# Attention block with group norm on one core: q and k of 512-token blocks by one level of Strassen's algorithm, with att kept in DRAM

## The chip, the cores and the metric

The kernel runs on one core of one Trainium2 chip. The metric is the device time of one execution in microseconds, as the median of several runs. Five engines work side by side, each with a queue of its own that it executes in order: TensorE (PE in the profile; PEld is its loading of weights), VectorE (DVE), ScalarE (ACT), GpSimd (POOL) and SyncE (SP), which here issues nearly all DMAs. Matrix products land in PSUM[...]; DVE and ACT read it, POOL works in SBUF only.

## The reference

The input x is 4 images of 512 channels by 48x48 = 2304 tokens, fp32.

```python
hn = group_norm(x)                                   # 32 groups of 16 channels
qkv = einsum('oc,bchw->bohw', qkv_w, hn) + qkv_b     # 3*512 rows, fp32
q, k, v = qkv as (b, 3, 8 heads, 64, 2304) in float16
w = softmax((q * 64**-0.25) . (k * 64**-0.25))       # 2304 x 2304 for each head
a = w . v                                            # back to float32, 512 channels
out = x + proj_w . a + proj_b
```

## The kernel before, in words

Work goes by **head pairs** (4 in each image, 16 in all, g = 0 to 15) and, inside a pair, by **blocks of 512 query tokens** (`QBLOCKS`: four of 512 and one of 256). Scores are computed transposed, key tokens on the partitions. For a block and a burst of 3 x 128 keys, `scores` (L920) issues the two heads' products into three PSUM tiles of two banks and one exponential of 1024 columns on ACT for each (L939). Two bursts later, `values` (L942) multiplies them with v. `add` (L968) sums the exponentials on DVE, in f16, into `acc` (3072 columns an instruction, L986, and two folds of 1024 at a block's end, L989). When a block is done, its row sums are formed on PE (`add_up`), copied (`rows`) and sent to 128 partitions by DMA, inverted on DVE (`invert`), written to DRAM and broadcast back (`spread`), and POOL multiplies (`divide`, L1071): att, f16, kept in SBUF, one tile of all tokens for each pair (`apool`, 7 buffers). `check_sums` on POOL watches the range of the sums; a general path, which is not entered for these inputs, follows if it fails.

The main loop (L1332) runs over a **stream** of 432 slots, 27 for each pair: a slot is one burst of scores, the `add` of the burst before, the values of two bursts before, and a `fill`.

The **side work** stands in one ordered list, `beside`: q and k of later pairs, v of later pairs and images, and the output projection of the image before. An entry (`piece`) has a nominal time in us, a function, marks for the first and last piece of a chain, a condition `when`, a slot before which it may not start (`after`), and the pair that needs it (`need`). `fill` (L1283) issues from the head of the list: credit grows in each slot by the rate that the deadlines ask, and a piece is taken while the credit covers half of it. After the last piece of a chain no new chain is begun in the same `fill`, because all chains in the stream share one PSUM bank (`ps_w`, one buffer). In the slot where a block's sums are formed, `fill` comes before the values, in the others after them.

A q or k chain (`qk_steps`, L695) is, for one part and one block, 4 channel chunks x 2 halves of 64 output rows, fp32, in a bank of 512 columns, given out in two pieces of 1.7 us nominal; DVE evacuates it with bias and scale (L719). The v chains (L743) have 256 columns an instruction. The projection (L833) takes att as fp32r, which ACT casts from the f16 tile (`att32`, L821), times the weights in two parts `whi` and `wlo`. `put_convert` enters the casts, at the earliest 8 slots (`BEHIND + 6`) after the block's last slot.

Group norm of the next image is done on DVE in place on x, which stays in SBUF as tiles of 128 channels by one block (`hn[b, c, j]`), as small `tasks` in `fill`; one step of it (a power, L631) is on POOL. Pair 0's q and k and half of the first image's v come before the stream, chains back to back in several banks.

Of the kernel before, what the change touches and what calls it, by code (L numbers as in the profile page):

```python
# [467 lines left out]
def fast_path(  # L468
# [19 lines left out]
    apool = ctx.enter_context(tc.tile_pool(name="apool", bufs=2 * NPAIR - 1))  # L488
# [91 lines left out]


    alone = [True]

    def chain_bank(name):
        if alone[0]:
            return ps_s.tile([P, 2, QB], F32, tag="ps", name=name)[:, 0, :]
        return ps_w.tile([P, QB], F32, tag="pw", name=name)
# [105 lines left out]
    qk = {}  # L693
# [46 lines left out]

    vv = {}
# [40 lines left out]
    normed = {}  # L782


    atts, res, at32 = {}, {}, {}

# [34 lines left out]
    def att32(b, j, pairs=range(NC)):  # L821
        o, n = QBLOCKS[j]
        for c in pairs:
# [7 lines left out]
            nc.scalar.copy(at32[b, j, c], atts[b * NPAIR + c][:, o : o + n])  # L831
# [53 lines left out]
    def proj_pieces(b, j):  # L885
# [19 lines left out]
        return [piece(0.0, begin)], chains  # L905
# [36 lines left out]
    def values(u):  # L942
# [5 lines left out]
        if k == 0:  # L948
            if j == 0:
                atts[g] = apool.tile([P, T], F16, tag="att", name=f"att_{g}")  # L950
            av[0] = ps_av.tile([P, QB], F32, tag="av", name=f"av_{g}_{j}")
# [119 lines left out]
    def divide(g, j):  # L1071
        o, n = QBLOCKS[j]
        nc.gpsimd.tensor_tensor(  # L1073
            atts[g][:, o : o + n],
            avx.pop((g, j))[:, :n],
            ibs.pop((g, j))[:, :n],
            ALU.mult,
        )

# [3 lines left out]
    def put(pieces, after=0, need=NG):  # L1083
        for p in pieces:
            p[5], p[6] = after, need
# [36 lines left out]
    def put_qk(g, part, blocks=range(NQ)):  # L1122

        for j in blocks:
            put(qk_chain(g, part, j), (g - 2) * per_pair - 1, g)
# [13 lines left out]
    def ready(b, j):  # L1139

        if b < B - 1:
            return BEHIND + 6
# [19 lines left out]

    for b in range(B):
        g = b * NPAIR
        old = b - 1
        if b == 0:
            for j in range(NQ):
                if j < NC:
                    put_run(load_wproj, j)
                if j > 0:  # L1170
                    put_run(split_wproj, j - 1)
                put_qk(g + 1, 1, (j,))
                put_qk(g + 1, 0, (j,))
            for block in SPARE:
                put_run(reload, *block)
        put_qk(g + 2, 1)
        put_qk(g + 2, 0)

        late = [j for j in range(NQ) if (b + 1, j) in SPARE]
        early = [j for j in range(NQ) if j not in late]  # L1180
        tiles = {j: range(o // P, (o + n) // P, 2) for j, (o, n) in enumerate(QBLOCKS)}
        for j in early:
            put_v(b, 1, tiles[j])
        if b == B - 1:
            put_qk(g + 3, 1)
            put_qk(g + 3, 0, range(NQ - 1))
            put_convert(old, 0)
            put_qk(g + 3, 0, (NQ - 1,))
# [12 lines left out]
            for j in (NQ - 2, NQ - 3, NQ - 1):  # L1201
                there = ends[(NG - 2) * NQ + j] + BEHIND + 6
                put_run(att32, b, j, FIRST, after=there)
# [9 lines left out]
        for j in early:  # L1213
            if j == NQ - 1 and b > 0:
                put_convert(old, 0)
            put_qk(g + 3, 1, (j,))
            put_qk(g + 3, 0, (j,))
            put_run(reload, b + 1, j)
        for j in late:
            put_v(b, 1, tiles[j])  # L1220
            put_qk(g + 3, 1, (j,))
            put_qk(g + 3, 0, (j,))
# [7 lines left out]
        put_qk(g + 4, 1)  # L1230
        put_qk(g + 4, 0)
        put_qk(g + 5, 1)
        put_qk(g + 5, 0)
# [49 lines left out]
    def fill(n):  # L1283


# [9 lines left out]
        do_tasks(room)  # L1295
        rate, work = 0.0, 0.0
        for us, _, _, _, _, _, need in beside:
            work += us
            left = min(need * per_pair, len(stream) - 4) - n
            rate = max(rate, work / max(left, 1))  # L1300
        credit[0] = min(credit[0] + rate, 4.0)
        closed = False
        while beside:
            us, _, first, last, when, after, _ = beside[0]
# [5 lines left out]
            closed = closed or last  # L1310

# [20 lines left out]
    for n in range(end):  # L1332
        now[0] = n
        while loads and loads[0][0] <= n:
            loads.popleft()[1]()
        summed = block_at(n - BEHIND - 1)
        if summed:
# [5 lines left out]
        if summed:  # L1343

            fill(n)
        if n >= BEHIND:
# [6 lines left out]
        if block_at(n - BEHIND - 4):  # L1353
# [116 lines left out]
```

## Time and profile before

| | |
|---|---|
| time before, median of 3 runs | 1617.96 us (1617.49 to 1618.23) |
| the profiled execution: time, span | 1618.91 us, 1617.1 us |
| mean granted TensorE clock | 0.999 |
| stream of 432 slots | from about 78 us to 1597 us, 3.5 us a slot |
| scores' exponentials on ACT (L939) | 1296, 1024 ns each, 950 ns apart |
| sum of exponentials on DVE (L986) | 349, 1750 ns each |
| att product on POOL (L1073) | 78, from 722 to 2822 ns |
| DMA | 82.1 MB, SP's queue 17.3% of the 16 engines |

The profile is one execution. In a row of instruction groups, "busy" is the time in which at least one of the group was at work, "mean ns of one" the mean duration, and the last part the idle time of that engine just before, with what ended it. In the timeline a row is: start in us, length in us, engine, line, operation, names written <- read, shapes, count, and in brackets the idle time before. The ends of matmuls are modelled; their starts are measured. Each fp32 matmul of the code appears as two instructions.

### The profile page before, as it was taken

To read this page: it belongs to the slowest core of one execution; us is meant where nothing else is said; L and a number is where in the kernel's file an instruction comes from. 1 tells how busy PE (TensorE), PEld (TensorE's weight loads), DVE (VectorE), ACT (ScalarE), POOL (GpSimd) and SP (SyncE) were. 2 spreads that over 40 slices of the span, in tenths; PEclk is the share of its full clock that TensorE was granted. 3 is DMA by queue.
4 is the path that set the end of the run, shared out by engine and by line. 5 is a ranking of instruction groups with operands and counts; after the bars stand their busy time and mean duration, and the time that the engine had idled before them with its cause. 6 is when DMAs were issued, how large, how long until landed. Compare 5 with 4: busy or idle time off the path is not lost.

```text
span 1617.1 us, 28315 instructions
## 1 busy us (share of the span) xinstructions
PE 1583.4 (98%) x11500; PEld 695.5 (43%) x11500; DVE 1136.2 (70%) x1302; ACT 1282.8 (79%) x1398; POOL 298.4 (18%) x419
## 2 busy tenths in 40 slices
PE   6999999999999999999999999999999999999996
PEld 2533434443333534555333353455533334434544
DVE  6267668866666678986666666898666666767775
ACT  3077777888888888888887887887888888888894
POOL 1001102211121222212111121111211131111211
PEclk9999999999999999999999999999999999999999
DMA  7002020000000023511000002352100000016424
GB/s 221 1 14 66 11 64 24 18 14 11 14 18 14 12 65 118 154 54 28 14 11 18 14 12 61 100 158 73 31 14 12 14 18 15 15 24 191 121 62 132
DMA packets 94898, 82.11 MB, mean 51 GB/s; under 512 B 50852, under 2 KB 60964, under 8 KB 94756
## 3 DMA queue, kind: packets, MB, share of 16 engines
q1 hardware_dynamic: 92724, 78.35, 17.3%
q8 instruction: 92, 1.51, 0.4%
q10 hardware_dynamic: 1904, 1.84, 0.4%
q14 instruction: 50, 0.41, 0.1%
q0 software_dynamic: 128, 0.01, 0.0%
HBM read 60.70 MB, written 19.17 MB: 49 GB/s over the span
## 4 chain that ended last, share of the span: by engine, by line
PE 91%; ACT 4%; issue 2%; DVE 1%; DMA 1%; POOL 0%; SPq 0%; ACTq 0%; DVEq 0%; POOLq 0%
PE pqk L709 29%; PE ps L932 19%; PE av L957 19%; PE pv L760 16%; PE pr L837 7%; ACT p L939 3%; PE ps L709 1%; PE sl L1009 1%; ACT a L831 1%; DMA x<-x_dram 1%; DVE acc L986 0%; DMA sums<-slx 0%; DVE r L860 0%; DMA row<-inv 0%; DMA ib<-row 0%
## 5 line engine op out<-in xcount | busy, mean ns | idle before, releaser
L939 ACT ACTIVATE p<-ps 128x1024 f16<-128x1024 f32 x1296 | 1231.9, 1027 | 299.9 <-PE ps L932 299.3
L986 DVE TENSOR_TENSOR acc<-acc,p 128x3072 f16<-128x3072 f16 x270 | 485.3, 1798 | 75.5 <-ACT p L939 74.7
L709 PE MATMUL pqk<-x,wqkv 128*64 128x512 f32 (+1 forms) x2464 | 519.3, 551 | 0.0
L932 PE MATMUL ps<-q,k 64*128 64x512 f16 (+1 forms) x2880 | 359.5, 358 | 6.2 <-ACT p L939 5.3
L957 PE MATMUL av<-p,v 128*64 128x512 f16 (+1 forms) x2880 | 361.0, 364 | 0.4 <-DVE slx L1025 0.3
L760 PE MATMUL pv<-wqkv,x 128*64 128x256 f32 x2304 | 268.6, 380 | 0.0
L709 PEld LDWEIGHTS pqk<-x,wqkv 128*64 128x64 f32 x2464 | 168.9, 137 | 224.2 <-issue 166.8
L1047 POOL TENSOR_SCALAR in<-sums 128x8 f32<-128x8 f32 (+1 forms) x158 | 116.6, 738 | 795.0 <-DMA sums<-slx 788.7
L932 PEld LDWEIGHTS <-k 64*128 64x128 f16 x2880 | 107.3, 94 | 286.1 <-issue 238.1
L957 PEld LDWEIGHTS <-v 128*64 128x64 f16 x2880 | 131.9, 109 | 210.8 <-issue 166.6
L1073 POOL TENSOR_TENSOR att<-avx,ib 128x512 f16<-128x512 f32 (+1 forms) x78 | 120.0, 1539 | 450.4 <-DMA ib<-row 406.3
L760 PEld LDWEIGHTS pv<-wqkv,x 128*64 128x64 f32 x2304 | 160.1, 137 | 92.8 <-issue 4.5
L986 DVE TENSOR_TENSOR acc<-p,p 128x3072 f16<-128x3072 f16 x79 | 138.2, 1749 | 0.0
L837 PE MATMUL pr<-a,whi 128*128 128x512 f32 (+1 forms) x312 | 122.2, 399 | 4.6 <-DVE r L860 3.2
L837 PE MATMUL pr<-a,wlo 128*128 128x512 f32 (+1 forms) x312 | 114.4, 373 | 0.0
L989 DVE TENSOR_TENSOR acc<-acc 128x1024 f16<-128x1024 f16 x156 | 108.4, 695 | 5.4
L719 DVE TENSOR_SCALAR q<-pqk,bqkv 128x512 f16<-128x512 f32 (+1 forms) x79 | 55.0, 696 | 80.4 <-PE pqk L709 79.8
L719 DVE TENSOR_SCALAR k<-pqk,bqkv 128x512 f16<-128x512 f32 (+1 forms) x75 | 52.2, 696 | 78.1 <-PE pqk L709 78.0
L768 DVE TENSOR_TENSOR v<-pv,bv 128x512 f16<-128x512 f32 x72 | 49.7, 691 | 81.1 <-PE pv L760 80.9
L966 DVE COPY avx<-av 128x512 f32<-128x512 f32 (+1 forms) x79 | 50.6, 641 | 66.4 <-PE av L957 66.4
L864 DVE SCALAR_TENSOR_TENSOR r<-pr,bproj,r 128x512 f32<-128x512 f32 (+1 forms) x80 | 54.9, 694 | 43.6 <-PE pr L837 43.0
L837 PEld LDWEIGHTS pr<-a,whi 128*128 128x128 f32 x312 | 58.5, 187 | 41.9 <-issue 18.7
(62 smaller groups left out, 448.8 us busy)
## 6 DMA issues: line engine op xcount, KB each, us to landing
r<-x_dram SPq DMA_DIRECT2D x72, 256.0 KB, 3.0
out_dram<-r SPq DMA_DIRECT2D x69, 256.0 KB, 2.1
ib<-row SPq DMA_DIRECT2D x126, 128.0 KB, 3.0
x<-x_dram SPq DMA_DIRECT2D x62, 256.0 KB, 4.3
x<-x_dram SPq DMA_DIRECT2D x16, 128.0 KB, 4.8
sums<-slx SPq DMA_DIRECT2D x128, 2.0 KB, 2.1
ib<-row SPq DMA_DIRECT2D x30, 64.0 KB, 3.0
wqkv<-qkv_wT_dram SPq DMA_DIRECT2D x2, 768.0 KB, 6.9
```

What stands on the lines that cost most here:

```text
L709: nc.tensor.matmul(pw[0][lo : lo + D, :n], wqkv[:, c, w0 + lo : w0 + lo + D], hn[b, c, j], start=(c == 0), stop=(c == NC - 1),)
L719: nc.vector.tensor_scalar(qk[g][part][:, o : o + n], pw[0][:, :n], bqkv[:, col : col + 1], SCALE, ALU.add, ALU.mult,)
L760: nc.tensor.matmul(pw[0][lo : lo + D, a, :], hn[b, c, i * P // QB][:, at + lo : at + lo + D], wqkv[:, c, 2 * C + half * C // 2 :][:, : C / ...
L837: nc.tensor.matmul(ps[:, :n], w[:, c, bass.ts(m, P)], at32[b, j, c], start=(i == 0), stop=(i == len(steps) - 1),)
L864: nc.vector.scalar_tensor_tensor(xt[:, i], places[i], bias, xt[:, i], ALU.add, ALU.add)
L932: nc.tensor.matmul(ps[:, h, a * n : (a + 1) * n], kt[rows, bass.ts(i, P)], qt[rows, o : o + n], start=True, stop=True,)
L939: nc.scalar.activation(pt[:, r], ps, AF.Exp)
L957: nc.tensor.matmul(av[0][lo : lo + D, :n], vv[b, pr // 2][:, i, pr % 2 * P + lo : pr % 2 * P + lo + D], pt[:, r, h, a * n : (a + 1) * n], ...
L986: nc.vector.tensor_tensor(t, before, pt, ALU.add)
L989: nc.vector.tensor_tensor(t[:, 0], t[:, 0], t[:, r], ALU.add)
L1047: nc.gpsimd.tensor_scalar(t, sm, limit, None, op)
L1073: nc.gpsimd.tensor_tensor(atts[g][:, o : o + n], avx.pop((g, j))[:, :n], ibs.pop((g, j))[:, :n], ALU.mult,)
```

## The change

For pairs 1 to 15, q and k of a 512-token block are no longer two chains of four chunks. The weights of q and k (2 x 128 rows by 512 channels) and the block of x (512 channels by 2 x 256 tokens) are taken as 2 x 2 matrices of blocks, and the four result blocks (q and k, each for the first and the second 256 tokens) come from seven products of 128 rows x 256 channels x 256 tokens, in Winograd's form: four sums of weights for each pair (`weight_sums`), four differences of x for each block (`x_sums`), both on POOL, and seven additions in the evacuation, by ACT, DVE and POOL. Two products share the bank at a time: `one` (p1, p2), `two` (p6, p7), `three` (p5, p3), and `four`, which takes p4 of two blocks. The 256-token block of each pair is computed as before, with q and k in one bank (`small_pieces`). q and k of a pair are entered in three groups of blocks (`GROUPS`), each piece a chain of its own.

Differences are prepared by `prepare` at the end of a `fill`, up to two items, at most one block ahead of the block whose turn it is; `ready_for` issues what is missing before the product that needs it. In a slot where `fill` comes after the values, a second `fill` is done before them if the credit is above 2.6. The credit's growth has moved into `pace`, once a slot.

att of all pairs but the last goes from POOL into a small f16 tile and by SP to DRAM; one tile of 512 columns by 4 chunks, `attl`, is fetched back for each block before `att32`, one fetch at a time. The division runs 5 slots after a block's values end in place of 4, and the casts start after `BEHIND + 9` slots in place of `BEHIND + 6`. The SBUF of `apool` goes from 7 buffers to 1, and holds the new tiles.

```diff
-    apool = ctx.enter_context(tc.tile_pool(name="apool", bufs=2 * NPAIR - 1))
+    apool = ctx.enter_context(tc.tile_pool(name="apool", bufs=1))
...
+    def weight_sums(g):
+        a11, a12, a21, a22 = (w_of(g, part, up) for part in (0, 1) for up in (0, 1))
+        s = [
+            work.tile([P, 2, P], F32, tag=f"s{i}", bufs=1, name=f"s{i}_{g}")
+            for i in range(4)
+        ]
+        nc.gpsimd.tensor_tensor(s[0], a21, a22, ALU.add)
+        nc.gpsimd.tensor_tensor(s[2], a11, a21, ALU.subtract)
+        nc.gpsimd.tensor_tensor(s[1], s[0], a11, ALU.subtract)
+        nc.gpsimd.tensor_tensor(s[3], a12, s[1], ALU.subtract)
...
+    def x_sums(k, which):
...
+            t = work.tile([P, 2, HALF], F32, tag=f"t{which}", name=f"t{which}_{g}_{j}")
...
+        for c in range(2):
+            nc.gpsimd.tensor_tensor(t[:, c], ins[0][c], ins[1][c], ALU.subtract)
...
+    def free(k, which):
+        if which == 0:
+            return k == 0 or (k - 1, 3) in sent
+        return k < 2 or (k - 2, {1: 3, 2: 4, 3: 2}[which]) in sent
...
+    def product(to, w, xs):
+        for c in range(2):
+            for lo in (0, D):
+                nc.tensor.matmul(
+                    to[lo : lo + D, :],
+                    w[:, c, lo : lo + D],
+                    xs[c],
+                    start=(c == 0),
+                    stop=(c == 1),
+                )
...
+        def scaled(engine, to, ps, other):
+            engine.scalar_tensor_tensor(to, ps, SCALE, other, ALU.mult, ALU.add)
+        def one(i, j):
...
+            p1, p2 = two_banks(f"p12_{g}_{j}")
+            product(p1, w_of(g, 0, 0), x_of(g, j, 0, 0))
+            product(p2, w_of(g, 0, 1), x_of(g, j, 1, 0))
...
+            nc.scalar.activation(t1, p1, AF.Identity, bias=bq[:, col], scale=SCALE)
+            scaled(nc.vector, qk[g][0][:, o : o + HALF], p2, t1)
+        def two(i, j):
+            k = first + i
+            ready_for(k, 2)
+            p6, p7 = two_banks(f"p67_{g}_{j}")
+            product(p6, weights[g][1], halves_of(parts[k, 2]))
+            product(p7, weights[g][2], halves_of(parts[k, 3]))
+            sent[k, 2] = True
+            x_sums(k, 4)
...
+            scaled(nc.vector, u2, p6, parts[k, "t1"])
...
+            nc.scalar.activation(u, p7, AF.Identity, bias=bkq[:, col], scale=SCALE)
+            nc.gpsimd.tensor_tensor(u, u, u2, ALU.add)
+        def three(i, j):
...
+            product(p5, weights[g][0], halves_of(parts[k, 1]))
+            product(p3, weights[g][3], x_of(g, j, 1, 1))
...
+            nc.scalar.activation(c5, p5, AF.Copy, scale=SCALE)
+            scaled(nc.vector, u4, p5, parts[k, "u2"])
+            scaled(nc.vector, qk[g][0][:, o : o + HALF], p3, u4)
...
+            nc.gpsimd.tensor_tensor(qk[g][1][:, o : o + HALF], c5, u, ALU.add)
+        def four():
+            banks = two_banks(f"p4_{g}_{js[0]}")
+            for i, p4 in enumerate(banks):
+                product(p4, w_of(g, 1, 1), halves_of(parts[first + i, 4]))
...
+            scaled(
+                nc.vector,
+                to[:, :, :HALF],
+                last_bank[0].rearrange("p (a t) -> p a t", a=2),
+                u3[0].rearrange("p (a t) -> p a t", a=2),
+            )
...
+    def fetch(b, j):
+        o, n = QBLOCKS[j]
+        t = work.tile([P, NC, QB], F16, tag="attl", bufs=1, name=f"attl_{b}_{j}")
+        pairs = NC - 1 if b == B - 1 else NC
+        nc.sync.dma_start(
+            t[:, :pairs, :n],
+            atd[b].rearrange("(c p) t -> p c t", p=P)[:, :pairs, o : o + n],
+        )
...
     def divide(g, j):
...
+            to = work.tile([P, QB], F16, tag="att", name=f"att_{g}_{j}")[:, :n]
         nc.gpsimd.tensor_tensor(
-            atts[g][:, o : o + n],
...
+            to, avx.pop((g, j))[:, :n], ibs.pop((g, j))[:, :n], ALU.mult
         )
+        if g < NG - 1:
...
+            at = atd[b][pr * P : (pr + 1) * P, o : o + n]
+            loads.append((now[0] + 1, lambda: nc.sync.dma_start(at, to)))
...
         if b < B - 1:
-            return BEHIND + 6
+            return BEHIND + 9
...
         if summed:
             fill(n)
+        elif beside and credit[0] > 2.6:
+            fill(n, False)
         if n >= BEHIND:
             values(stream[n - BEHIND])
```

## The prediction

> **What bounds the kernel now.** I read the page first: busy shares, chain, groups.
>
> ```profile
> PE 1583.4 (98%) x11500; PEld 695.5 (43%) x11500; DVE 1136.2 (70%) x1302; ACT 1282.8 (79%) x1398; POOL 298.4 (18%) x419
> ...
> PE 91%; ACT 4%; issue 2%; DVE 1%; DMA 1%; POOL 0%; SPq 0%; ACTq 0%; DVEq 0%; POOLq 0%
> ```
>
> TensorE (PE) is busy for 98% of the span and carries 91% of the chain that ended last; its own waits come to some 24 us, half of them one wait at the start. A matmul saved shortens the run, as long as no other engine makes PE wait. POOL is nearly free.
>
> A busy time cannot price a matmul, because matmuls overlap. I price them by the spacing of the evacuations in the opening, where chains run back to back (timeline of the first 110 us):
>
> ```profile
> 41.73 0.75 DVE L719 TENSOR_SCALAR q<-pqk,bqkv 128x512 f16<-128x512 f32 x1 [2.68 <-PE pqk L709]
> ...
> 45.16 0.75 DVE L719 TENSOR_SCALAR q<-pqk,bqkv 128x512 f16<-128x512 f32 x1 [2.68 <-PE pqk L709]
> ...
> 57.24 0.69 DVE L768 TENSOR_TENSOR v<-pv,bv 128x512 f16<-128x512 f32 x1 [2.76 <-PE pv L760]
> 60.70 0.69 DVE L768 TENSOR_TENSOR v<-pv,bv 128x512 f16<-128x512 f32 x1 [2.76 <-PE pv L760]
> ```
>
> A q chain is 4 chunks x 2 halves of 64 output columns, and the trace has two instructions for each fp32 matmul: 16 instructions of 512 columns in 3.43 us, 215 ns each. A v chain is 32 instructions of 256 columns in 3.45 us, 108 ns each. So 256-column instructions with the same 64-column fp32 weights, which is what the change issues, cost half: their weight loads stay hidden.
>
> Then one slot of the stream in the middle of q and k work (timeline, 374 to 392 us):
>
> ```profile
> 386.57 2.85 ACT L939 ACTIVATE p<-ps 128x1024 f16<-128x1024 f32 x3 [0.44 <-PE ps L932]
> ...
> 386.83 0.84 PE L957 MATMUL av<-p,v 128*64 128x512 f16 x6
> ...
> 387.50 1.88 PE L709 MATMUL pqk<-x,wqkv 128*64 128x512 f32 x8
> ...
> 389.32 0.82 PE L932 MATMUL ps<-q,k 64*128 64x512 f16 x6
> 389.44 0.75 DVE L719 TENSOR_SCALAR q<-pqk,bqkv 128x512 f16<-128x512 f32 x1 [1.52 <-PE pqk L709]
> 389.75 2.85 ACT L939 ACTIVATE p<-ps 128x1024 f16<-128x1024 f32 x3 [0.32 <-PE ps L932]
> ```
>
> A slot is three score tiles, one piece of side work and the value matmuls of two slots before. With one piece (8 instructions of 512, about 1.72 us) it lasts 3.24 us (386.08 to 389.32); in it ACT works 2.85 us and waits 0.32 to 0.44 us for scores. That 0.4 us is all the room ACT has. DVE starts on a chain only after its last matmul, and its sum of 1.75 us sits in the same queue.
>
> The last reading is how POOL and DVE stand to each other (timeline, 300 to 330 us):
>
> ```profile
> 317.45 1.75 DVE L986 TENSOR_TENSOR acc<-acc,p 128x3072 f16<-128x3072 f16 x1
> ...
> 317.73 2.60 POOL L1073 TENSOR_TENSOR att<-avx,ib 128x512 f16<-128x512 f32 x1 [4.22 <-DMA ib<-row]
> ...
> 319.12 1.69 DVE L660 TENSOR_SCALAR x<-x,ga,gb 128x256 f32<-128x256 f32 x2
> ```
>
> The POOL product needs 1.27 us alone. Here it takes 2.60: it starts during DVE's sum (which ends at 319.20) and gets 1.13 us of progress only afterwards. Then the two DVE instructions queued at 319.12 take 1.69 us in place of 0.73.
>
> **What the Trainium skill says.** *SBUF — State Buffer*, "Who interferes with whom": a VectorE instruction with two SBUF inputs, or in a two-port mode, and a GpSimd instruction that reads SBUF exclude each other, and the second waits for the whole of the first. The lines above agree: 1.33 us lost. *GPSIMD Engine Reference*, "3.1 Elementwise — side-by-side cycle accounting": a two-input GpSimd operation needs about 2.6 cycles an element. Trace: 732 ns for 256 columns, 1267 for 512, so 2.09 ns an element and 197 ns fixed, a little better. *ScalarE: Activation LUTs*, "What ACT_TABLE_LOAD costs": 186 ns + 0.833 ns a column, 93 more for each pointer operand, 93 of overlap between neighbours. Trace: 585 by that rule for the 256-column normalisation with two pointers, 586 measured. *TensorE: Matmul & The Clock Gate*, "Wait — 56ns, not 53.3ns?": columns / 2.4 + 2.5 ns; 215.8 and 109.2 against the 215 and 108 above.
>
> **The change, part by part.**
>
> *Matmuls.* Fifteen head pairs (all but the first) have four 512-token blocks each: 60 blocks. Before: 2 parts x 16 instructions of 512 = 32 x 215 = 6.87 us. After: 7 products x 2 chunks x 2 halves x 2 = 56 instructions of 256, 56 x 108 = 6.04 us. Saved 0.83 us x 60 = **50 us**, all on PE. The 256-token blocks keep their matmuls and only share a bank.
>
> *ACT.* Three 256-column evacuations a block (t1, u, c5), by the skill's rule 493, 493 and 399 ns, less the overlap 400, 400, 306: 1.1 us x 60 = +66 us. No row prices an activation from PSUM of this size; the nearest, the 256-column cast from SBUF, is 421 ns. Bounds: 0.3 to 0.5 us each. Most new chains carry one, so ACT does 2.85 + 0.37 = 3.22 us in a slot of 3.24. It is hidden by a hair; 2 chains in 14 ("four") carry none and the v and projection slots give room back, and three score banks let ACT lag some 0.7 us. Over the run: 1283 + 66 = 1349 of about 1580, 85%.
>
> *DVE.* Per block it loses 2 evacuations of 750 ns and gets four of 256 columns, two-input from PSUM, 478 ns (the row of the 256-column residual), and half of one of 512 (750): 1.50 becomes 2.29 us, x 60 = +47 us, to 1183. Hidden by PE, until waits on POOL are added.
>
> *POOL.* Per block 8 differences and 2 sums of 256 columns, and 4 weight sums a pair: 660 x 0.73 = +480 us, to about 780 without waits. A slot of 3.24 us has 5/6 of a 1.75 us sum, 0.23 us of folding and some 0.1 us of normalisation on DVE's side: about 1.8 us taken. POOL wants 10 x 0.57 us in 6.5 slots, plus the division and check (1.6 us in 6), about 1.15 of the 1.4 us left. It fits, with about 20% to spare. Cost to DVE: an add that finds POOL at work waits up to 0.57 us; about 500 such instructions x 0.2 = 100 us, so DVE comes to 1280 of 1580, 81%.
>
> *New waits.* All side chains share one PSUM bank. Before, a 512 chain held it over two slots; now a chain fills and is emptied within each. After "one" the bank is free only after ACT's t1 (behind three exponentials) and a DVE step, about 1.0 us after the chain's end; the next chain starts 1.4 us after it (386.08 to 387.50 in the trace). So 0.4 us of slack, 0.1 after "three" (two DVE steps). Behind a late DVE step stands the next sum, then the next evacuation. Where the new second fill puts a chain before the values, the other follows within 0.8 us and must wait about 0.7. Pieces: 29.5 of 1.72 us in 27 slots a pair, so doubles are few. Between pairs POOL must do 4 weight sums and 6 differences after the old pair's last "three" and before the new pair's first "two", five slots on: 10 operations at about 2.5 a slot. Bounds for all this: 0 to 0.35 us a chain over 210 chains (0 to 73 us), of which I take 0.07 (15 us); 0 to 2 us at each of 15 pair changes (0 to 30), of which I take 0.4 (6 us). No reason suggests a gain here.
>
> *att through DRAM.* 75 stores of 128 KB or less and 20 fetches of up to 512 KB join SP's queue: 18 MB more on 82, DMA share 17% to 21%, 95 issues of about 0.4 us. The division runs one slot later and its store a slot after that, the sums' DMA a slot later again, so SP is held only if POOL is over a slot late; then DVE's reciprocal, which waits for the sums, is held too. Converts start three slots later (9 for 6), covered by other pieces where the queue has any; two slots are given to each fetch, against 3 to 5 us for loads of 256 KB. Taken as 0, bounds 0 to 10 us. The group scale's power on POOL (0.7 us) now stands behind differences: 0 to 3 us, three times, taken as 0. The last pair's att stays in SBUF, so the end is unchanged.
>
> Sum: -50 + 15 + 6 = -29 us on the profiled execution's 1618.9 (span 1617.1 + 1.8 around it), 1590. The median shown is 1 us below that execution, within rounding: **1590**.
>
> **Rivals.** (1) *Everything hides.* PE stalls for no more than now: 1618 - 50 = 1568, with a few doubles 1573. For it: the slack of each stage is positive by the numbers above. Against: four engines end within 0.4 us of each other in a slot. (2) *The shared port turns the bound over.* POOL's differences delay DVE's sums, these delay evacuations, and PE waits at the single bank before each chain, or at "two" for differences that POOL has not finished. The saving is spent at 50 / 210 = 0.24 us a chain; a full wait for one POOL operation (0.57 us) less the 0.25 us of slack, 0.32 us, gives 67 us of stalls: 1635. For it: the 2.60 and 1.69 us above. Against: before, the 63 products of 512 columns already average 1691 ns for 1267, and PE shows no wait that leads to them. (3) *ACT saturates.* If its step takes 0.55 us, a slot is 3.4 us rather than 3.24: 0.16 x 180 = 29 us on top, 1619 with my stalls, no change. (4) *The saving is not there*, because 256-column products do not run at 108 ns: against it stand 2304 such v instructions.
>
> **How the numbers follow.** Forecast case (1578 to 1606) 0.48; everything hides, below 1578, 0.22; ACT or DVE taking most of the saving, 1606 to 1622, 0.13, a third of it within 0.2% (3.2 us, about what a measurement of this kernel can tell from no change); the shared port, above 1622, 0.17. Faster 0.76, same 0.05, slower 0.19. The range runs from 1571 (all hidden) to 1628, into the port case.
>
> **What would show it.** Right: 32 x 60 instructions of 512 replaced by 56 x 60 of 256 near 108 ns, PE's busy time down by about 50 us and its share down to 96 or 97%; ACT near 1350, POOL near 800, DVE sums on average 0.1 to 0.3 us longer. Wrong: PE waits for DVE evacuations or for POOL's differences of over 50 us in sum, or ACT without gaps through the q and k slots.

## The result, and the profile after

| | before | after |
|---|---|---|
| time, median | 1617.87 us (1617.49 to 1618.23) | **1761.7 us** (1757.91 to 1766.51) |
| ratio, 95% interval | | **1.0891** (1.0864 to 1.0918): slower |
| profiled execution: time, span | 1618.91, 1617.1 us | 1762.06, 1760.1 us |
| mean granted TensorE clock | 0.999 | 0.978 |
| stream of 432 slots, start of the first to start of the last | 1516.5 us | 1662.1 us |

Forecast were 1590 us, with a range of 1571 to 1628; the run is 144 us slower than before. First the busy shares of the changed kernel (the page's first part):

```profile
PE 1590.8 (90%) x12940; PEld 826.9 (47%) x12940; DVE 1231.6 (70%) x1452; ACT 1342.0 (76%) x1578; POOL 1010.2 (57%) x1082
```

PE went from 98% of its span to 90%. ACT's 1342 us and DVE's 1232 us are what the prediction summed up (1349, 1183 to 1280), and neither is full: the bound has not passed to another engine. PE has become an engine that waits. (The chain of what ended last can be followed back over only 1% of this span; what follows rests on waits, timeline and slots.)

The waits of the changed kernel: engine, instruction, what ended the wait; us in sum, times, longest.

```profile
DVE u4q L863 <- ACT p L907: 97.6, 52, 3.0
...
ACT u3k L893 <- DVE u2q L863: 75.4, 57, 6.8
...
DVE q L863 <- ACT t1q L876: 52.8, 45, 2.9
PEld p L835 <- ACT u3k L893: 41.6, 33, 2.7
...
PE p L835 <- DVE q L863: 36.3, 35, 6.2
...
PE p L835 <- ACT u3k L893: 25.2, 19, 2.2
...
PE p L835 <- POOL t L797: 4.7, 4, 1.8
```

ACT and DVE wait for one another inside one evacuation, and products (`p`, L835) wait for the last step of the evacuation of the pair of products before. They hardly wait for the differences themselves (4.7 us, and 11.1 us before their weight loads).

Now the timeline, a slot of undisturbed length and the long one after it:

```profile
449.13 4.44 POOL L797 TENSOR_TENSOR t<-x,x 128x256 f32<-128x256 f32 x2
...
450.99 0.82 PE L1185 MATMUL ps<-q,k 64*128 64x512 f16 x6
451.04 1.94 DVE L1239 TENSOR_TENSOR acc<-acc,p 128x3072 f16<-128x3072 f16 x1
451.21 0.47 ACT L893 ACTIVATE u3k<-p,bkq 128x256 f32<-128x256 f32 x1 [0.42 <-DVE u2q L863]
...
453.52 1.27 POOL L1331 TENSOR_TENSOR att<-avx,ib 128x512 f16<-128x512 f32 x1
...
454.24 0.82 PE L1185 MATMUL ps<-q,k 64*128 64x512 f16 x6
...
454.83 0.33 SPq L1338 DMA_DIRECT2D attd<-att  x1
...
456.53 0.38 SPq L1070 DMA_DIRECT2D attl<-attd  x1
457.01 1.14 SPq L1281 DMA_DIRECT2D sums<-slx  x2
...
460.95 0.20 DVE L1307 RECIPROCAL inv<-sums 128x8 f32<-128x8 f32 x1 [7.97 <-DMA sums<-slx]
...
461.51 0.42 DVE L863 SCALAR_TENSOR_TENSOR q<-p,u4q 128x256 f16<-128x256 f32 x1
...
462.08 3.68 PE L835 MATMUL p<-x,wqkv 128*64 128x256 f32 x16 [6.25 <-DVE q L863]
```

The slot from 450.99 to 454.24, with 16 instructions of 256 columns, lasts 3.25 us: as long as the 3.24 us with 8 instructions of 512 before, so the price per instruction is right. The trouble begins in it. Two differences take 4.44 us (449.13 to 453.57) in place of 1.4 because DVE's sums hold the port. Behind them POOL's att product (453.52) is late. The store of att stands in SP's queue ahead of the sums' DMA and leaves only at 454.83; a fetch of att between the two then waits for that store to land (456.53). So the sums' DMA is issued only at 457.01, DVE's reciprocal waits 7.97 us for it, and behind the reciprocal in DVE's queue stands the evacuation that PE needs: in the next slot PE waits 6.25 us.

The 16 instructions after the wait then last 3.68 us in place of 1.89, at half the clock. The table by stretches of the changed kernel, "us, busy us of PE, PEld, DVE, ACT, POOL, PEclk, DMA share, GB/s":

```profile
446.00:459.00 13.00, 9.69 (x84) 4.84 (x79) 5.09 (x5) 10.62 (x13) 12.21 (x13) 1.00 0.13 31
459.00:465.50 6.50, 3.42 (x16) 1.92 (x16) 2.62 (x4) 0.00 (x0) 4.29 (x7) 0.50 0.27 83
```

The Trainium skill, *TensorE: Matmul & The Clock Gate*, "What's actually happening", says that an idle window of about 3.4 us halves TensorE's clock and that a busy one restores it. The trace agrees on the half clock and on the length: in the stream there are 14 spells at 0.50, 3.4 or 6.8 us each, 68 us in sum; before there is none. It differs on how much idling is needed. The spells begin on a fixed grid of 3.41 us; in the stretch of 3.41 us just before each of them the profile has PE idle for 1.8 to 3.2 us, and in no other full-clock stretch of the stream for more than 1.7. So a wait of some 2 us can be enough, and it is then paid again in part: here 3.42 us of PE work at half clock, 1.7 us lost on top of the 6.25. In all the spells PE was at work for 52.5 us; half of that, about 26 us, is my estimate of what they cost the stream.

The groups that answer to the lock shown before (busy, mean ns of one):

```profile
L1239 DVE TENSOR_TENSOR acc<-acc,p 128x3072 f16<-128x3072 f16 x270 | 504.5, 1869 | 30.0 <-ACT p L1192 29.4
...
L797 POOL TENSOR_TENSOR t<-x,t 128x256 f32<-128x256 f32 x240 | 257.4, 1093 | 112.1 <-PE p L835 111.6
...
L1242 DVE TENSOR_TENSOR acc<-acc 128x1024 f16<-128x1024 f16 x156 | 149.6, 959 | 5.4
```

Alone a difference takes 0.72 us, here 1093 ns or more on average. DVE's sums went from 1798 to 1869 ns on average (the 1750 ns ahead of the prediction is the median), the folds from 695 to 959, the first sum of a block from 1749 to 1843: 270 x 71 + 156 x 264 + 79 x 94 ns = 68 us lost on DVE.

### The profile page after: what moved, and what is told of

Read it like the earlier page. It is cut to its first block, busy times and chain, and to the rows that moved or that the text cites. A ratio compares the mean times of both kernels' runs of the same rounds, so it can differ in the third digit from the quotient of the medians.

```text
span 1760.1 us, 32708 instructions
## 1 busy us (share of the span) xinstructions
PE 1590.8 (90%) x12940; PEld 826.9 (47%) x12940; DVE 1231.6 (70%) x1452; ACT 1342.0 (76%) x1578; POOL 1010.2 (57%) x1082
## 5 line engine op out<-in xcount | busy, mean ns | idle before, releaser
L1239 DVE TENSOR_TENSOR acc<-acc,p 128x3072 f16<-128x3072 f16 x270 | 504.5, 1869 | 30.0 <-ACT p L1192 29.4
L1185 PE MATMUL ps<-q,k 64*128 64x512 f16 (+1 forms) x2880 | 369.0, 360 | 13.2 <-ACT p L1192 11.3
L797 POOL TENSOR_TENSOR t<-x,t 128x256 f32<-128x256 f32 x240 | 257.4, 1093 | 112.1 <-PE p L835 111.6
L1300 POOL TENSOR_SCALAR in<-sums 128x8 f32<-128x8 f32 (+1 forms) x158 | 95.8, 606 | 342.9 <-DMA sums<-slx 334.3
L835 PE MATMUL p<-t,s 128*64 128x256 f32 x1440 | 180.9, 386 | 40.3 <-ACT u3k L893 25.2
L1242 DVE TENSOR_TENSOR acc<-acc 128x1024 f16<-128x1024 f16 x156 | 149.6, 959 | 5.4
L835 PEld LDWEIGHTS p<-t,s 128*64 128x64 f32 x1440 | 102.2, 138 | 108.1 <-ACT u3k L893 41.6
L1239 DVE TENSOR_TENSOR acc<-p,p 128x3072 f16<-128x3072 f16 x79 | 145.6, 1843 | 0.9 <-ACT p L1192 0.9
L797 POOL TENSOR_TENSOR t<-x 128x256 f32<-128x256 f32 x120 | 134.5, 1140 | 0.0
L835 PE MATMUL p<-x,wqkv 128*64 128x256 f32 x960 | 117.5, 387 | 16.5 <-DVE q L863 13.0
L797 POOL TENSOR_TENSOR t<-x,x 128x256 f32<-128x256 f32 x120 | 131.0, 1111 | 1.6 <-DVE x L668 1.6
```

The source lines that it names most:

```text
L797: nc.gpsimd.tensor_tensor(t[:, c], ins[0][c], ins[1][c], ALU.subtract)
L835: nc.tensor.matmul(to[lo : lo + D, :], w[:, c, lo : lo + D], xs[c], start=(c == 0), stop=(c == 1),)
L1185: nc.tensor.matmul(ps[:, h, a * n : (a + 1) * n], kt[rows, bass.ts(i, P)], qt[rows, o : o + n], start=True, stop=True,)
L1239: nc.vector.tensor_tensor(t, before, pt, ALU.add)
L1242: nc.vector.tensor_tensor(t[:, 0], t[:, 0], t[:, r], ALU.add)
L1300: nc.gpsimd.tensor_scalar(t, sm, limit, None, op)
```

## The experiments

They take the change apart. Each time is the median of two or four executions, each ratio is to the kernel before on the same chip (1618.4 to 1618.9 us). Lengths of stretches, slots and waits come from the one profiled execution of each kernel.

### First: one suspect at a time

**Plain chains.** In `group_pieces`:

```diff
-        return wino_pieces(g, js) if len(js) == 2 else small_pieces(g, *js)
+        return [p for j in js for part in (1, 0) for p in qk_chain(g, part, j)]
```

> The change with its q and k put back to plain chains (two of 512 columns for each block); att in DRAM, the later casts, the second fill and the pace stay. Three theories for the 192 us by which the stream of slots is longer than its matmuls ask. A (the store): att's store stands in SP's queue until POOL, late with differences of x, has divided; the DMA of the next block's sums is behind it, DVE waits for the sums and everything waits for DVE. B (POOL's load): the differences are not ready or keep the shared port from DVE. C (the bank): ACT and DVE read one bank in turn, so each waits in its queue for the other, and the one bank comes free late. All three need the seven products: each expects 1620 to 1640 here, the old time and a few us for the fetches at the end. If att in DRAM were itself the cause, the time would stay above 1690.

Measured: 1680.4 us, 1.0381 (1.035 to 1.0411). Without anything of Strassen, the rest of the change (att in DRAM, later casts, second fill, `pace`) costs 62 us. The prediction took it as nothing.

**Store of att later**, so that SP doesn't hold the sums' DMA behind a late POOL:

```diff
-            loads.append((now[0] + 1, lambda: nc.sync.dma_start(at, to)))
+            stores.append((now[0] + 5, lambda: nc.sync.dma_start(at, to)))
...
-            return BEHIND + 9
+            return BEHIND + 13
```

(fetches four slots later too)

> The change with att's store issued five slots after the division in place of one (fetches and casts four slots later accordingly), so that POOL has divided before SP comes to the store and nothing stands behind it. A: DVE's waits for the sums (34 us in 7 pieces) go, with the slow-clock spells after them: 1700 to 1720. B and C: only the late divisions are gone, within 15 us of 1762.

Measured: 1753.7 us, 1.0833 (1.0791 to 1.0876), against 1.0891 (1.0864 to 1.0918). SP's waits, of the changed kernel and of this one:

```profile
SPq L1338 <- POOL att L1331: 501.3, 69, 19.1
```

```profile
SPq L1339 <- POOL att L1332: 21.4, 5, 7.3
```

480 us of SP's waiting go and the run gains 8, with intervals that overlap. Two effects cancel in this. In pairs 1 to 13 (slots 27 to 377) the stream is 23.6 us shorter than in the changed kernel, and DVE's waits for the sums fall from 34.0 us (7 times) to 8.2 (3 times). From the last pair's first slot to the end the run is 12.8 us longer: the first of the last five fetches is issued in slot 416 in place of 412, so that slots 412 to 415 have no side work and the projections are bunched behind them. So the hold shown at 454.83 costs some 24 us of the stream, an estimate that the run's total hides; it is a twentieth of what SP waits in sum.

**No differences.** The products read blocks of x where the change reads differences:

```diff
...
-        for c in range(2):
-            nc.gpsimd.tensor_tensor(t[:, c], ins[0][c], ins[1][c], ALU.subtract)
-        parts[k, which] = t
+        parts[k, which] = x_of(g, j, which > 2, which % 2)
```

> The change without the differences of x: the products take blocks of x in their place, and the scale of q and k is a quarter, so q and k are not the reference's, and the check of the sums has no consequence. POOL loses 480 of its 660 new instructions; matmuls, ACT and DVE stay. B: the products and DVE's sums no longer wait for POOL: 1580 to 1620. A: POOL divides in time, so the gain is that of the late store and little more: 1690 to 1720. C: bank and evacuations are as they were, so 1690 to 1720 as well, with PE's waits for DVE and ACT before products still there.

Measured: 1695.8 us, 1.0475 (1.0445 to 1.0506): the differences cost 66 us.

**Evacuations on DVE**: t1, u and c5 by `nc.vector.tensor_scalar` in place of `nc.scalar.activation`.

> The change with t1, u and c5 evacuated by DVE in place of ACT, so that DVE alone reads the bank. C: the waits of ACT for DVE (75 us) and of DVE for ACT (150 us) go, the bank is free sooner and the time falls to 1690 to 1720, although DVE does 70 us more. A and B: DVE's extra work makes it no better, 1760 to 1790.

Measured: 1759.8 us, 1.0871 (1.0839 to 1.0902): no difference. Taking these steps off ACT gains nothing where DVE takes them up.

### Second: the schedule, and the number of steps

**Casts ahead.** The cast of att before a projection is marked as the last piece of a chain, so that the projection isn't released in the same fill; on plain chains and on the change (the three early casts of the last image likewise):

```diff
-        return [piece(0.0, begin, when=when)], chains
+        return [piece(0.0, begin, last=True, when=when)], chains
```

> Plain chains with att in DRAM (1680), and the cast entered as the last piece of its fill, so that its projection starts one slot later at the earliest. Theory D (the cast): since the cast waits for a fetch, it and its projection are let go in one fill, and PE stands behind the cast, which stands behind three exponentials on ACT: some 3 us of waiting, and after it 3 to 7 us at half the clock, at each of 20 fetches. D expects 1625 to 1650. Rival: the fetches themselves come too late (one buffer, one fetch at a time), PE runs out of side work in the last pair whatever the order: 1665 to 1680.

> The change itself with the cast entered as the last piece of its fill. D: the same gain as with plain chains, 30 to 50 us: 1710 to 1730. Rival (fetches too late): within 15 us of 1760.

Measured: 1668.4 us, 1.0305 (1.0265 to 1.0344) on plain chains, 12 us less than without; 1751.7 us, 1.0819 (1.0788 to 1.0851) on the change, 10 less. The place is the last pair. In the changed kernel:

```profile
1644.71 1.70 ACT L1061 CAST a<-attl 128x512 fp32r<-128x512 f16 x3
1645.42 0.79 PE L1089 MATMUL pr<-a,whi 128*128 128x512 f32 x1 [2.86 <-ACT a L1061]
...
1646.43 0.36 SPq L1070 DMA_DIRECT2D attl<-attd  x1
1646.44 0.63 PE L1089 MATMUL pr<-a,whi 128*128 128x512 f32 x1
1646.87 0.63 PE L1089 MATMUL pr<-a,wlo 128*128 128x512 f32 x1
```

PE waits 2.86 us for the first cast, and the projection then runs at half clock (some 425 ns from one start to the next; 233 from 1650.26 on).

**One evacuation.** No differences, and each pair of products emptied by one DVE `tensor_scalar` of 512 columns:

> The kernel without differences (1696), and each pair of products evacuated whole by one DVE instruction of 512 columns, as a plain chain is; t1, u, c5, the sums on POOL and the further DVE steps are left out, so q and k are not the reference's. Left are the seven products in chains of one slot each. Theory C (the hand-over of the bank, ACT after exponentials and DVE after ACT, comes later than the next chain's start): 1630 to 1645, 62 us of it att in DRAM less 48 us of matmuls. Rival: a chain in every slot on one bank is too tight by itself, whoever empties it: 1675 to 1695.

Measured: 1646.4 us, 1.0169 (1.0139 to 1.0198), 49 us less than with the steps.

**No second fill** in the change:

```diff
-        elif beside and credit[0] > 2.6:
-            fill(n, False)
```

> The change without the second fill ahead of the values. C: two chains in one slot wait for the bank, so taking them away gains 5 to 20 us unless the work that is left over piles up at the pairs' ends, where it is issued without pause. Rival: that pile costs more: 1765 to 1800.

Measured: 1721.8 us, 1.0634 (1.0603 to 1.0665): 40 us for two lines. The trace has 11 slots without any side work in the change, 5 without the second fill. Seven of the 11 lie in the last pair (five of them in slots 417 to 428), where only projections are left and none is released before its fetch is two slots old; two of the 5 do. Of the 43 us by which the stream is shorter, the last pair gives back 25. The first pair gives 12: with the second fill its slots 5 and 17 hold two chains of products each and last 7.0 and 7.1 us, where in the kernel before a slot with two pieces takes 4.96.

### Third: the ladder, all without the second fill

> Plain q and k chains of 512 columns, att in DRAM with its store, fetch and later casts, and no second fill before the values: against the kernel before, only att in DRAM and the bookkeeping of the rate remain. The question is whose the 62 us of the plain chains (1680) were. Theory A, the second fill: it spends the side work early and leaves the slots of the last pair bare, and a pair's late casts are then waited for; without it the stream is again even and the run takes 1618 to 1630. Theory B, the transfer of att: stores and fetches in SP's queue and casts that wait for them cost most of the 62, and the run stays at 1655 to 1680.

> The seven products alone: no differences and no sums of x or u on POOL, each pair of products emptied by one DVE instruction of 512 columns (the other steps of the combination are left out, so q and k are not the reference's), no second fill. Theory of the schedule: with the second fill, the differences and the steps gone, the 50 us of matmuls should appear: about the time of plain chains without the second fill less 46 to 50, so 1570 to 1585 if that one is near 1620. Rival, the shorter chains themselves (a bank filled and emptied within a slot, 14 groups where there were 8) cost PE time: 1600 to 1630.

> No differences of x on POOL (the products take blocks of x in their place, so q and k are not the reference's), evacuations in steps as in the change, no second fill. If the costs add, 1696 - 40 = 1656 us, and the steps of the evacuation are then worth this run less the one with one evacuation (expected about 50 to 70). If the second fill's cost was mostly a collision with POOL's lateness, the gain without it is under 25 us here: 1670 or more.

| kernel, each without the second fill | us | ratio (95%) | step |
|---|---|---|---|
| before | 1618.9 | | |
| plain chains, att in DRAM | 1636.4 | 1.0107 (1.009 to 1.0124) | +17.5 |
| seven products, one evacuation, no differences | 1606.6 | 0.9923 (0.9907 to 0.994) | -29.8 |
| the same, evacuation in steps | 1653.2 | 1.0217 (1.02 to 1.0234) | +46.6 |
| with the differences (the run above) | 1721.8 | 1.0634 (1.0603 to 1.0665) | +68.6 |
| with the second fill (the change) | 1761.7 | 1.0891 (1.0864 to 1.0918) | +39.9 |

The terms hardly depend on each other: the second fill costs 44 us on plain chains, 40 with one evacuation, 43 without differences; the differences 66 with it and 69 without; the steps 49 and 47. The saving is there: the row with one evacuation beats the kernel before by 0.8%, though it leaves most of the combination out. The next row, still without the differences, has lost it.

Where the steps lie in the stream, read from the traces: mean length of a slot, from its first score product to that of the next slot, for slots with the same work (number of them in the change's schedule in brackets; side work of 16 instructions of 256 columns or 8 of 512).

| | one q and k piece (173) | one v piece (91) | block's end, one q and k piece (30) |
|---|---|---|---|
| before | 3.24 | 3.26 | 3.46 |
| plain chains | 3.24 | 3.26 | 3.49 |
| one evacuation | 3.29 | 3.27 | 3.70 |
| in steps | 3.44 | 3.26 | 4.13 |
| with differences | 3.55 | 3.39 | 4.89 |

The steps cost 173 x 0.15 + 30 x 0.43 = 39 of the 47 us; the differences 173 x 0.11 + 91 x 0.13 + 30 x 0.76 = 54 of the 69. The slots at a block's end, where `fill` stands before the values, lose most each. The timeline of the kernel in steps without differences:

```profile
920.39 1.95 PE L821 MATMUL p<-x,wqkv 128*64 128x256 f32 x16
921.94 2.37 DVE L1228 TENSOR_TENSOR acc<-acc 128x1024 f16<-128x1024 f16 x2
...
922.43 0.47 ACT L862 ACTIVATE t1q<-p,bq 128x256 f32<-128x256 f32 x1 [0.36 <-PE p L821]
...
924.23 0.41 DVE L849 SCALAR_TENSOR_TENSOR q<-p,t1q 128x256 f16<-128x256 f32 x1
...
924.70 1.95 PE L821 MATMUL p<-x,s 128*64 128x256 f32 x16 [0.84 <-DVE q L849]
```

The chain's products end at 922.27, t1 is ready at 922.90, but DVE is in two folds, lengthened to 2.37 us by POOL's att product, and takes its step at 924.23; PE waits 0.84 us for the bank.

**Three mends of the schedule together** (no second fill, cast ahead, store later) on the change:

> The change as it is, with three edits of its schedule: no second fill, casts entered as a last piece so that a projection is not released in the same fill, the store of att four slots later. Alone these gave 40, 10 and 8 us. If they are separate costs the run takes about 1762 - 58 = 1704; if the second fill was behind the other two (the late casts of the last pair are the same gaps), 1715 to 1722.

Measured: 1711.6 us, 1.0576 (1.0558 to 1.0594): 50 us less than the change, 10 less than without the second fill alone. The later fetches take back a part here too: against the run without the second fill, pairs 1 to 13 are 20.9 us shorter, the last pair and the end 8.0 longer. It is the fastest run of the whole change, and still 93 us behind the kernel before. A later store without later fetches at the end was not tried.

### Fourth: how the differences and the steps cost

**Differences made, but read by nobody**, and **POOL as busy, but only writing**:

```diff
-        parts[k, which] = t
+        made[k, which] = t
+        parts[k, which] = x_of(g, j, which > 2, which % 2)
```

```diff
-        for c in range(2):
-            nc.gpsimd.tensor_tensor(t[:, c], ins[0][c], ins[1][c], ALU.subtract)
+        nc.gpsimd.memset(t, 1.0)
+        nc.gpsimd.memset(t, 1.0)
+        nc.gpsimd.memset(t[:, 0], 1.0)
```

> The change without the second fill (1721.8 us), with the differences of x made on POOL as before but read by nobody: the products read blocks of x, so q and k are not the reference's. Theory of the port: POOL's reading makes DVE wait and DVE's evacuations come late; nothing changes for that here, so 1700 to 1722. Rival, the products wait for differences (and POOL for products before it may overwrite them): it goes to within 10 us of the run without differences, 1653 to 1665.

> As the run with unread differences, but each pair of differences of 2 x 726 ns is replaced by three fills of a constant (512, 512 and 256 elements; from the rows of 8 and 96 elements 563 + 563 + 350 = 1476 ns): POOL is as busy and as late for its other work, but it reads nothing. Theory of the port: most of the cost goes, 1655 to 1675, and DVE's sums come back from 1870 to about 1790 ns. Rival, POOL's lateness (att, its store, SP's queue, the reciprocal behind it): the cost stays, 1690 to 1720.

Measured: 1719.3 us, 1.0622 (1.0595 to 1.0649), unread; 1660.2 us, 1.0265 (1.0248 to 1.0282), writing only. Nobody needs the differences here and they cost as much as ever, 66 us over the kernel without them (1653.2); with the same instructions' time spent in writing, 7. So what costs is POOL's reading of SBUF. DVE's groups, first of the kernel with unread differences, then of the one that only writes:

```profile
L1242 DVE TENSOR_TENSOR acc<-acc,p 128x3072 f16<-128x3072 f16 x270 | 509.9, 1889 | 27.1 <-ACT p L1195 26.4
L1245 DVE TENSOR_TENSOR acc<-acc 128x1024 f16<-128x1024 f16 x156 | 150.7, 966 | 5.4
```

```profile
L1243 DVE TENSOR_TENSOR acc<-acc,p 128x3072 f16<-128x3072 f16 x270 | 486.9, 1803 | 30.6 <-ACT p L1196 30.1
...
L1246 DVE TENSOR_TENSOR acc<-acc 128x1024 f16<-128x1024 f16 x156 | 127.8, 819 | 5.3
```

The rows are back at those of the kernel without differences (1788 and 821 ns). The Trainium skill, *SBUF — State Buffer*, "Who interferes with whom", says just this: a VectorE instruction with two SBUF inputs contends with a GpSimd one that reads SBUF, not with one that only writes. What stays open is by which way the 59 us between the two runs reach PE. The fills aren't lengthened themselves (three in 532 + 528 + 316 = 1376 ns, against 2 x 1.1 us), so POOL is also less late for its other work: SP's waits for its att product fall from 489 to 375 us, and DVE's for the sums from 33.0 to 15.1. That way, through SP's queue, costs some 21 us beside the differences, by the run with three mends; the rest may be DVE's late steps.

**The same subtractions beside plain chains**: 480 of 256 columns (of weights, read by nobody), one or two at the end of each slot from the 27th on.

```diff
+        if n >= 27:
+            for i in range((n - 26) * 480 // 405 - (n - 27) * 480 // 405):
+                t = work.tile([P, HALF], F32, tag="t9", bufs=2, name=f"t9_{n}_{i}")
+                a, z = wqkv[:, i, :HALF], wqkv[:, i + 2, :HALF]
+                nc.gpsimd.tensor_tensor(t, a, z, ALU.subtract)
```

> Plain q and k chains, att in DRAM, no second fill (1636.4 us), and 480 POOL subtractions of 256 columns (of two blocks of weights, read by nobody), one or two at the end of each slot from the 27th on. Theory that POOL's reads delay every DVE result that PE waits for: as beside the products, 1690 to 1705. Rival, they cost that much only where a bank is filled and emptied within a slot by several steps; a chain of 16 instructions over two slots has some 1.4 us of room: 1640 to 1660.

Measured: 1655.5 us, 1.0219 (1.0202 to 1.0236), 19 us over plain chains. DVE's rows:

```profile
L1239 DVE TENSOR_TENSOR acc<-acc,p 128x3072 f16<-128x3072 f16 x270 | 512.5, 1898 | 61.9 <-ACT p L1192 61.3
L1242 DVE TENSOR_TENSOR acc<-acc 128x1024 f16<-128x1024 f16 x156 | 145.8, 934 | 5.4
```

Over plain chains without them (1778 and 712 ns) DVE loses 270 x 120 + 156 x 222 ns = 67 us, no less than beside the short chains (270 x 101 + 156 x 145 + 79 x 116 ns = 59 us). The same delay of DVE goes with 66 us where each slot fills and empties the bank, and with 19 where a chain runs over two slots: its slots stay at 3.24 us. The comparison isn't clean. The subtractions here are spread evenly and those of the change come in bunches, and SP's waits for POOL hardly rise here (249 us, 241 without the subtractions), so that the hold in SP's queue, some 21 of the 66 us, is missing. How much of the rest is the bunching wasn't tried.

**Steps on DVE** (t1, u, c5; no differences, no second fill), and **steps without POOL's two sums** (c5 goes straight to k, u is not summed):

> Seven products, no differences, no second fill, evacuation in steps (1653.2 us), with t1, u and c5 on DVE instead of ACT. q and k are not the reference's, since blocks of x stand for the differences. Theory of the order on one bank: DVE's steps no longer wait behind ACT's exponentials (92 + 50 us of such waits) nor ACT for DVE (42 us); ACT loses 58 us of work and DVE gains some 65; the run gains 15 to 40: 1613 to 1638. Rival, the number of steps in a row at the bank and DVE's load: no gain, 1645 to 1665.

> Seven products, no differences, no second fill, evacuation in steps (1653.2 us), with POOL's two sums a block left out: c5 goes from ACT straight to k, and u is not summed (q and k are not the reference's). 120 POOL operations of 1.35 to 1.6 us go. Theory of the port, at the price of the differences (59 us for 480 operations, 0.12 us each): 15 us gained, 1638. Rival, the bank's hand-over from engine to engine is the whole cost: 1649 to 1655.

Measured: 1653.5 us, 1.022 (1.0203 to 1.0237), and 1645.9 us, 1.0155 (1.0135 to 1.0175), against 1653.2 us with both. On DVE the plain slots get shorter (3.36 for 3.44 us), which fits ACT and DVE waiting for each other there, but block ends get longer (4.52 for 4.13), probably because all steps now stand behind the folds: my expected 15 to 40 us failed. POOL's sums are worth 7 us (half of the price that I had from the differences). What stays, 39 us, is the price of several steps in a row at one bank, on whichever engine; the number of steps and the work queued ahead of each were not separated.

**Plain chains with the store later and casts ahead**, no second fill:

> Plain chains with att in DRAM and no second fill (1636.4 us), with the store four slots later and each cast a last piece. If the 17 us are SP's queue and projections released together with their casts, 1620 to 1628; if they are the later casts themselves (9 slots after a block for 6, thinner side work at the image changes), 1632 to 1642.

Measured: 1640.4 us, 1.0134 (1.0117 to 1.0151): no gain on 1636.4, with intervals that overlap. Again two effects cancel. The stream is 11.8 us shorter than without the two edits and only 4.4 us longer than before; but what follows the start of its last slot takes 39.2 us in place of 24.1 (22.8 before), since the last fetches come about four slots later and more of the projection is left over (66 instructions after that start, for 24). In pairs 1 to 13 the edits gain 2.4 us, so SP's hold and the release in one fill cost little there with plain chains. Without the two edits the stream is about 17 us longer than before in pairs 2, 6 and 9 to 11 and 6.6 us in the last, and a little shorter elsewhere. Whether later casts, the transfers or the new `pace` make the 17.5 us stays open.

## Why the prediction was wrong, point by point

The sum was -50 + 15 + 6. Its first term holds; what failed is the price of everything around the matmuls. The waits at the bank and for POOL, taken as 21 us, cost about 135: some 20 for the shorter chains, 46.6 for the steps, 68.6 for the differences. Two terms were put at nothing: the second fill, which cost 39.9 us, and att through DRAM, 17.5.

- **Matmuls, -50 us: right.** Undisturbed slots with 16 instructions of 256 columns are as long as those with 8 of 512, and the step from plain chains to seven products is -29.8 us though it already has shorter chains in one bank (slots of 3.29 for 3.24 us, block ends of 3.70 for 3.49).
- **Durations of the new instructions: right or a little high.** t1 and u take 473 ns and c5 407 (taken: 493 and 399), the two-input steps about 0.42 us (478), a difference 0.72 alone (0.73). DVE's lock waits came to 68 us (about 100 taken). The sums of ACT and DVE held, and said little about the time. POOL came to 1010 us rather than 800.
- **The signs named beforehand.** PE's busy time was to fall by about 50 us; it rose from 1583.4 to 1590.8, and the half clock is some 26 of the 58 us between. PE's waits for evacuations before products, 36.3 + 25.2 us in the rows above, passed the 50 us that were to show the forecast wrong; the other sign, waits for POOL's differences, stayed away.
- **att through DRAM, "taken as 0, bounds 0 to 10 us": failed.** It cost 17.5 us. That SP might be held, with DVE's reciprocal behind it, was named and does happen (7.97 us at 460.95). Beside the differences this hold costs 21 to 24 us of the stream, beside plain chains 2.4, so it is not what makes the 17.5; what does stays open.
- **The second fill, "doubles are few": failed, the plainest miss.** They are few: five slots hold two chains of products. But I priced them by the bank alone, 0.7 us a double, and these slots last 5.7 to 7.8 us where a slot with two pieces took 4.96 before. The larger part acts through the queue: the second fill spends side work early and leaves the last pair bare. 40 us in all, outside every bound that I gave.
- **Bank waits, 15 us of 0 to 73: mis-sized.** The steps cost 46.6 us and the shorter chains some 20 more (the 50 us of the first term, less 29.8). I had summed the steps' durations with ACT's and DVE's queues independent. But ACT and DVE may not read one bank together (the Trainium skill, *PSUM — Partial Sum Buffer*, "PSUM bank collisions raise a hardware error", asks for a semaphore by bank), and the trace shows the hand-over: u waits for u2, u4 for c5, 173 us in the first two rows of waits. Yet moving the steps to one engine didn't help: the row of steps counts, not the hand-over alone.
- **Differences on POOL: the rival's mechanism was right, its weight wrong.** Rival 2 said 67 us of stalls through the shared port and DVE's late evacuations. The differences cost 66 to 69, 59 of them through POOL's reading, but some 21 of that by a way that the rival didn't name, the late store in SP's queue. I gave it 0.17, because PE showed no wait that led to the port before. My reading of this, which the runs support but don't prove: before, the wait was absent because a chain over two slots had 1.4 us of room, and the change takes that room away. The plain chains beside the same subtractions, 19 us for the same delay of DVE, point to it.
- **POOL "fits, with about 20% to spare": wrong in effect.** It has time in sum (57%), but a difference lasts 1.1 us on average.
- **ACT saturates (rival 3), the saving is not there (rival 4): no.** Evacuations on DVE changed nothing; the row of the ladder with one evacuation is faster than before.
- **Not foreseen at all:** the clock. 68 us of the stream at half speed, about 26 us lost. They are a part of the terms above, not one more.

The forecast took the edits with no matmul in them as free and the slack of before as given. The sum that was measured is 17.5 - 29.8 + 46.6 + 68.6 + 39.9 = 143 us. None of the runs points to a whole version that beats the kernel before: the steps of the combination, without any differences, already leave it 2.2% behind.

## What to carry to other kernels

A shorter product pays only if what empties it is as short: count the steps in a row between the last matmul into a bank and the first of the next, with everything queued ahead of each step, before counting flops. An engine that delays another can cost nothing as long as a buffer has room for the delay, so "no wait leads there now" is no evidence once the change takes that room. Price the small scheduling lines of a diff too: here two of them cost nearly as much as the matmuls could save. And an edit that takes one wait away can bring another elsewhere: read its effect by stretches of the run before calling it small, as with the later store.

## What the runs showed of the hardware that I had not expected

- In the changed kernel, each of the 14 spells of 3.4 or 6.8 us at a granted clock of 0.50 follows a stretch of 3.41 us, on a fixed grid, in which TensorE was idle for 1.8 us or more; up to 1.7 us of idling in such a stretch left the clock full.
- POOL filling a tile with a constant (528 ns for 512 columns) delays DVE's two-input sums by 15 ns on average, POOL subtracting (346 us if undisturbed, against 330 of filling) by 101.
- 480 us less of waiting in SP's DMA queue shortened pairs 1 to 13 by 24 us, and 26 us of DVE's waiting went with it.
